# Quantising, a decay's scan, a weight load and gathers moved inside a joint pipeline of an eight-layer kernel

## The chip, the cores and the metric

The kernel runs on one core of a Trainium2 chip. The metric is device time in microseconds (us) for one execution; four runs of the kernel before gave 1078.79 to 1080.51 us, median 1079.82. The engines are TensorE (PE in the profile; PEld is its weight load), VectorE (DVE), ScalarE (ACT), GpSimd (POOL) and SyncE (SP, which issues most transfers). GpSimd issues the transfers of its own queue, among them the gathers by index.

## The reference, cut to what matters

The input `x` is 16 x 128 x 256: 16 sequences ("batches" b here) of 128 tokens with 256 features; `ctx` has the same shape. Four layers follow one another, each a cross-attention-like block and a feed-forward block, all with residuals and tanh gates. The change lies in the stretch from layer 1's attention to layer 2's first block, and in the load of the weights of layer 2's experts:

```python
def _L1_ffn_ref(x, w1, w2, w3):
    def act_quant(x):
        scale = 127.0 / jnp.clip(jnp.max(jnp.abs(x), axis=-1, keepdims=True), EPS)
        return jnp.clip(jnp.round(x * scale), -128.0, 127.0) / scale
    def weight_quant(w):
        scale = 1.0 / jnp.clip(jnp.mean(jnp.abs(w)), EPS)
        return jnp.clip(jnp.round(w * scale), -1.0, 1.0) / scale
    def bitlinear(x, w):
        return jnp.einsum('bsd,hd->bsh', act_quant(x), weight_quant(w))
    h = jax.nn.silu(bitlinear(x, w1)) * bitlinear(x, w3)
    return bitlinear(h, w2)

def _L2_xattn_ref(q, k, v, decay):          # k = v = ctx, q = layernorm(x)
    kv = kh * vh
    def step(r, inc):
        r = d * r + inc
        return (r, r)
    _, rs = jax.lax.scan(step, r0, kv_t)    # along the 128 tokens
    out = qh * jnp.moveaxis(rs, 0, 1)

x = x + jnp.tanh(g_ffn[0])   * _L0_ffn_ref(_layernorm(x), ...)      # 8 experts, top 2
x = x + jnp.tanh(g_xattn[1]) * _L1_xattn_ref(_layernorm(x), ctx, ctx, mask, Wq, Wk, Wv, Wo)
x = x + jnp.tanh(g_ffn[1])   * _L1_ffn_ref(_layernorm(x), w1, w2, w3)
x = x + jnp.tanh(g_xattn[2]) * _L2_xattn_ref(_layernorm(x), ctx, ctx, decay)
x = x + jnp.tanh(g_ffn[2])   * _L2_ffn_ref(_layernorm(x), ...)      # 8 experts, top 2
```

The weights w1 and w3 are 256 x 704, w2 is 704 x 256. Each is scaled by the mean of its absolute values, rounded and clipped to -1, 0 or 1. Since layer 2's keys and values are both `ctx`, its recurrence runs over the squares of `ctx`, with one decay per head of 16 channels.

## The kernel before, in words

Channels or tokens of one batch lie on 128 partitions. `xg` holds the running x, `ctxT` holds `ctx` with channels on partitions, as two halves c of 128 channels, each with 16 x 128 columns (batch after batch). The stages run in order: layer 0's block, its experts (`stage_moe0`), then a joint pipeline (`stage_l1x` with `following`), then layer 2's experts (`stage_moe2`) and layer 3.

**The joint pipeline** is the loop over n from -4 to 22 in `stage_l1x`. In step n it gathers the expert outputs of batch n+4 and takes its statistics (`stats`, which calls `collect`), normalises it, and runs the attention of batch n: queries (`tq`, L1041), scores (`s`, L1083), exponentials (`pt`, L1086), the mix with values (`av`, L1092; `avs`, L1094), and one step later `normalise` (transposes `ta`, L1100; the rows L1102 to L1105, which end with the tile `o`), `turn_o` (`to`, L1111; `oT`, L1113) and `output` (`y`, L1120; L1122). Two steps later the batch is done, and pairs q of two batches enter the following stages. The function `then(m, place)` is called at four places (0 to 3) of each step; the table `order` says which function of pair q runs at which place. A key (d, place) means step m = 3 + d + 2q. So pair q has statistics in step 3+2q at place 3 (L1294 to L1297, the power on GpSimd), scaling and the largest value in step 4+2q at place 0 (L1303 to L1315), rounding on ScalarE (`rounded`, L1320) at place 1, transposes (`fx`, L1328, L1329) at place 3, the two products with w1 and w3 in step 5+2q (`fu`, L1339; silu, L1346; L1347; L1356 to L1363), rounding and transposing of the hidden values in step 6+2q (L1367; `fh`, L1374; L1375), w2 in step 7+2q at place 2 (`fy`, L1381; L1386), and layer 2's block, `retain`, in step 8+2q (`fr`, L1401, transposes of ctxT; L1404, L1405).

**Preparation.** `follow` begins with the loads of w1, w3 and w2 as float32 into one tile `raws` (the slot of layer 0's expert weights), in whose rest GpSimd writes `dk[0]`, 2048 columns of ones with a zero at the start of each batch. `begun(n)` is called once in each step n >= 0, at its end but before place 3, and hands out the rest: step 0 lays out small buffers; steps 1 to 3 sum the absolute values of one weight each (`total`, L1236); steps 1 and 2 also square one half of ctxT on ScalarE (L1257); step 3 computes the scales (`size`: the matmul `ts`, L1240, over partitions and L1241 to L1243); step 4 quantises w1 and w3 and step 5 w2, with three VectorE operations for each (`integers`, L1251 to L1253); step 6 and step 7 each multiply `dk[0]` by the decay of one half (L1260) and scan that half in one operation over all 2048 columns (L1263), the zeros restarting it at each batch; step 8 issues the six loads of layer 2's expert weights (`moe2_weights`, L134 and L140) into the slot that `raws` gives up.

**Order.** TensorE, VectorE and ScalarE execute in the order in which the code is written (`manual_schedule`); GpSimd and SyncE get an order from the scheduler. Every engine takes its own instructions one after another. `fetcher` keeps three buffers `yc`; `collect(b)` asks for batch b and b+1, each by two indirect gathers on GpSimd's queue (L707), and adds them with L726.

Of the kernel before, what the change touches and what calls it, by code (L numbers as in the profile page):

```python
# [10 lines left out]
F32 = mybir.dt.float32  # L11
BF16 = mybir.dt.bfloat16
F32R = mybir.dt.float32r
AF = mybir.ActivationFunctionType
ALU = mybir.AluOpType
# [3 lines left out]
P = 128  # L19
B = 16  # L20
D = 256
# [34 lines left out]
def passage(ctx: ExitStack, tc: tile.TileContext, a: dict, out: bass.AP, inv, flag):  # L56
# [69 lines left out]

    def moe2_weights():

        t = mow.tile([P, (E + 1) * WE], F32R, name="L2we", tag="mw")
        v = t.rearrange("p (e w) -> p e w", e=E + 1)  # L130
        for n, s in ((0, "w1"), (1, "w3")):
            for c in range(2):
                at = (2 * c + n) * I
                nc.gpsimd.dma_start(  # L134
                    v[:, :, at : at + I], a[f"L2_{s}"][c * P : (c + 1) * P].rearrange("p (e i) -> p e i", e=E + 1)
                )
        w2 = a["L2_w2"]
        for n in range(2):
            at = 4 * I + n * D
            nc.gpsimd.dma_start(  # L140
                v[0:HI, :, at : at + D],
                bass.AP(tensor=w2.tensor, offset=w2.offset + n * HI * D, ap=[[D, HI], [I * D, E + 1], [1, D]]),
            )
        return t


    def layernorm(pool, g, extra=None, tag="xn"):
# [569 lines left out]
    def collector(pool, ys, pos, wgt):  # L717

        fetch = fetcher(pool, ys, pos, 3)

        def collect(b):
            y = fetch(b)
            fetch(b + 1)
            xv = xg[b // GB][:, b % GB, :]
            for i in range(2):
                nc.vector.scalar_tensor_tensor(xv, y[:, i, :], wgt[:, i, b : b + 1], xv, ALU.mult, ALU.add)  # L726

        return collect
# [440 lines left out]
    def following(sh, dcol):  # L1169
# [5 lines left out]

        def follow(pss, pst):


            raws = mow.tile([P, (E + 1) * WE], F32, name="raws", tag="mw")
            cut = [6 * D * i for i in range(4)]  # L1180
            flat = [raws[:, cut[i] : cut[i] + n * width] for i, (_, n, width) in enumerate(sizes)]
            for (name, n, width), raw in zip(sizes, flat):
                nc.sync.dma_start(
                    raw.rearrange("p (n w) -> p n w", n=n), a[f"L1_ffn_{name}"].rearrange("(n p) w -> p n w", p=P)
                )
            dk = [raws[:, cut[3] + i * B * P : cut[3] + (i + 1) * B * P] for i in range(2)]
            nc.gpsimd.memset(dk[0], 1.0)
            nc.gpsimd.memset(dk[0].rearrange("p (b s) -> p b s", b=B)[:, :, 0:1], 0.0)
            v = {}
            wq = []  # L1190

            def layout():

                t = sh.tile([P, 2 * B * P], F32, name="follow", tag="xT", bufs=1)
                at = [0]

                def take(name, n, *shape):
                    u = t[:, at[0] : at[0] + n]
                    at[0] += n
                    if shape:  # L1200
                        names = "abc"[: len(shape)]
                        u = u.rearrange(
                            f"p ({' '.join(names)}) -> p {' '.join(names)}", **{k: d for k, d in zip(names, shape)}
                        )
                    v[name] = u

                take("xn", 2 * D, 2, D)
                for i in range(2):
                    take(f"sil{i}", HID // 2)
                    take(f"hid{i}", 6 * P)  # L1210
                    nc.gpsimd.memset(v[f"hid{i}"][:, HID:], MAGIC)
                at0 = at[0]
                take("xT", 2 * P)
                v["xT"] = v["xT"].bitcast(BF16).rearrange("p (c s) -> p c s", c=2)
                for i in range(2):
                    take(f"hT{i}", 3 * P)
                    v[f"hT{i}"] = v[f"hT{i}"].bitcast(BF16).rearrange("p (n s) -> p n s", n=6)
                take("sum", 6, 3, 2)
                take("step", 3)
                take("s2t", 1)  # L1220
                take("magic", 2)
                for i, x in enumerate((MAGIC, -MAGIC)):
                    nc.gpsimd.memset(v["magic"][:, i : i + 1], x)
                for r in range(2):
                    for f in "fr":
                        take(f"st{f}{r}", 12, 2, 6)
                        take(f"mv{f}{r}", 4, 2, 2)
                        take(f"ve{f}{r}", 2)
                        take(f"rs{f}{r}", 2)
                    take(f"am{r}", 2)  # L1230
                    take(f"iv{r}", 2)
                    take(f"a13{r}", 4, 2, 2)
                    take(f"hm{r}", 6, 3, 2)
# [4 lines left out]
            def size():  # L1238
# [3 lines left out]
                nc.vector.reciprocal(v["sum"][:, :, 1], v["step"])  # L1242
                nc.vector.tensor_scalar(v["s2t"], v["step"][:, 2:3], tg[:, 5:6], 1.0 / 127.0, ALU.mult, ALU.mult)  # L1243

            def integers(i):
                name, n, width = sizes[i]
                if i == 2:
                    w = kv1.tile([P, n, width], BF16, name="w2q", tag="k3")
                else:
                    w = sh.tile([P, n, width], BF16, name=f"{name}q", tag="sil")  # L1250
                nc.vector.tensor_scalar(flat[i], flat[i], v["sum"][:, i, 1:2], MAGIC, ALU.mult, ALU.add)  # L1251
                nc.vector.tensor_scalar(flat[i], flat[i], MAGIC, 1.0, ALU.subtract, ALU.min)
                nc.vector.tensor_scalar(w.rearrange("p n w -> p (n w)"), flat[i], -1.0, None, ALU.max)  # L1253
                wq.append(w)

            def squared(c):
                nc.scalar.activation(ctxT[:, c, :], ctxT[:, c, :], AF.Square)  # L1257

            def decayed(c):
                nc.vector.tensor_scalar(dk[1], dk[0], dcol[:, c : c + 1], None, ALU.mult)  # L1260

            def scanned(c):
                nc.vector.tensor_tensor_scan(ctxT[:, c, :], dk[1], ctxT[:, c, :], 0.0, ALU.mult, ALU.add)  # L1263

            def begun(n):
                if n == 0:
                    assert not work
                    layout()
                elif n < 4:
                    total(n - 1)  # L1270
                    if n < 3:
                        squared(n - 1)
                    else:
                        size()
                elif n == 4:
                    integers(0)
                    integers(1)
                elif n == 5:
                    integers(2)
                elif n < 8:  # L1280
                    decayed(n - 6)
                    scanned(n - 6)
                elif n == 8:
                    l2we.append(moe2_weights())

            def x_of(q):
                b = 2 * q
# [108 lines left out]
            def retain(q):  # L1396
# [19 lines left out]
                (3, 1): [lambda q: turn_hidden(q, 0)],  # L1416
                (3, 2): [lambda q: turn_hidden(q, 1)],
                (4, 2): [down],
                (5, 0): [lambda q: stats(q, "r")],
                (5, 1): [retain_normal],  # L1420
                (5, 3): [retain],
# [511 lines left out]
    with tc.tile_pool(name="kv1", bufs=1) as kv1:  # L1933
        vbuf = kv1.tile([P, B, 4, 32], F32, name="v", tag="k0")
        ka = kv1.tile([P, B, P], F32, name="ka", tag="k1")
        anyk = kv1.tile([P, B], F32, name="anyk")
        stage_l0x(ka, vbuf, anyk)
        l0s = moe0_shared()
        l0g = col_chunks("l0g", a["L0_gw"], E)
        cn = sorter(kv1)  # L1940
        kept = pos, wgt, cn, xs, ys
        l1k = col_chunks("l1k", a["L1_wk"], P)
        l1v = col_chunks("l1v", a["L1_xattn_Wv"], 64)
        l1q = col_chunks("l1q", a["L1_wq"], 512)
        l1o = col_chunks("l1o", a["L1_xattn_Wo"], D)
        dcol = load("dcol", [P, 2], a["dcol"])
        l2g = col_chunks("l2g", a["L2_gw"], E)
        l2b = load("l2b", [P, E], a["L2_ffn_gate_b"].partition_broadcast(P))
        l3w = l3_weights()
        l3r = col_chunks("l3r", a["L3_wr"], E)  # L1950
        l3br = load("l3br", [P, E], a["L3_ffn_br"].partition_broadcast(P))
        with tc.tile_pool(name="mow", bufs=1) as mow:
            l0w = moe0_weights()

            l2we = []
            work = [
                lambda _, ps, p=p: keys_values(p, ps, ka, vbuf, anyk, l1k, l1v) for p in range(B // 2)
            ]
            with tc.tile_pool(name="sh", bufs=2) as sh:
                stage_moe0(l0w, *l0s, l0g, 4, sh, *kept, work)  # L1960
                with tc.tile_pool(name="yc", bufs=3) as yc:
                    stage_l1x(l1q, l1o, ka, vbuf, collector(yc, ys, pos, wgt), work, following(sh, dcol))
            stage_moe2(kv1, l2we[0], l2g, l2b, 6, *kept)
    with tc.tile_pool(name="l3fw", bufs=1) as fw:
        l3a = col_chunks("l3a", a["L3_A"], 512, fw)
        l3B = col_chunks("l3B", a["L3_B"], D, fw)
# [92 lines left out]
```

## Time and profile before

The times of one profiled execution and of the runs shown:

| what | us |
|---|---|
| median of four runs (1078.79 to 1080.51) | 1079.82 |
| the profiled execution | 1075.64 |
| its span, first to last instruction | 1073.9 |
| TensorE / VectorE / ScalarE / GpSimd busy in the span | 900.2 / 612.4 / 450.8 / 341.0 |
| row L1105 of the first step that writes it (n = 1) | starts 363.56 |
| the same row in step 4, 8, 12, 16 | 393.04, 456.41, 504.65, 547.01 |
| first row of layer 2's experts on VectorE (L750) | starts 582.06 |

In the page's second part the span is cut in 40 slices of 26.8 us; a digit is the busy share of an engine in tenths, and PEclk is the granted clock of TensorE in tenths of full speed. The joint pipeline lies in slices 13 to 21:

```profile
PE   3899978899999978788964858998169999998797
...
DVE  5988867322225568876778586444445555534442
ACT  1211024223322546467662242455257777882111
POOL 5766322643124322421011046550533332201000
PEclk9999989999999988899997557899579999997999
```

A row of the timeline gives its start and duration, engine, line and operation, then the tile written, the tiles read and the shape; in brackets stands how long the engine was idle before it and what ended the wait. A row of a group ends with busy time and the mean in ns of one instruction. "follow" is the tile of small buffers of `following`.

GpSimd's own rows, where the loads of layer 2's weights stand among small operations and gathers:

```profile
443.83 1.13 POOL L134 DMA_DIRECT2D L2we<-in_L_w_dram  x1 [8.60 <-DVE ctxT L1263]
445.01 0.73 POOL L1297 TENSOR_TENSOR follow<-follow,neghalf 128x2 f32<-128x2 f32 x1
445.71 1.05 POOL L134 DMA_DIRECT2D L2we<-in_L_w_dram  x1
...
453.87 2.11 POOL L140 DMA_DIRECT2D L2we<-in_L_w_dram  x2 [0.85 <-issue]
456.28 1.08 POOL L707 DMA_INDIRECT yc<-ys,pos  x1 [0.30 <-issue]
```

### The profile page before, as it was taken

Reading aid. Unit: us, or ns where it says so; the run is one execution under the profiler, and the core shown is the slowest. Engines: PE = TensorE matmul, PEld = TensorE weight load, DVE = VectorE, ACT = ScalarE, POOL = GpSimd, SP = SyncE. Lnnn points to the kernel's source line nnn. Section 1 sums busy time; section 2 is a strip of 40 time slices with the busy share of each in tenths; the row PEclk is TensorE's granted clock in tenths of the full one; section 3 lists DMA queues with packets and bytes.
Section 4 is the critical chain, followed back from the end, with each engine's and each line's share of the span. In section 5 each row is a group of like instructions: output and inputs, shape, how many; then the busy total and the mean of one; then the engine's idle time right before and its main releaser. Section 6 shows DMA issues by size and latency. Waiting matters only on the chain. (4 is left out here: it accounts for less than half of the span.)

```text
span 1073.9 us, 14873 instructions
## 1 busy us (share of the span) xinstructions
PE 900.2 (84%) x5212; PEld 600.1 (56%) x5212; DVE 612.4 (57%) x1528; ACT 450.8 (42%) x690; POOL 341.0 (32%) x387
## 2 busy tenths in 40 slices
PE   3899978899999978788964858998169999998797
PEld 1444456677778434454543757887145555555564
DVE  5988867322225568876778586444445555534442
ACT  1211024223322546467662242455257777882111
POOL 5766322643124322421011046550533332201000
PEclk9999989999999988899997557899579999997999
DMA  9100070233341100870000102352588787520000
GB/s 305 41 1 1 0 221 20 65 107 104 78 137 47 40 20 20 136 66 1 1 1 15 64 1 89 118 141 79 151 238 237 220 221 194 166 76 1 20 31 32
DMA packets 71401, 94.12 MB, mean 88 GB/s; under 512 B 9271, under 2 KB 63127, under 8 KB 69015
## 3 DMA queue, kind: packets, MB, share of 16 engines
q1 hardware_dynamic: 56952, 67.21, 21.0%
q0 software_dynamic: 14080, 23.78, 10.9%
q10 hardware_dynamic: 288, 2.10, 0.5%
q8 instruction: 45, 0.74, 0.3%
q14 instruction: 36, 0.29, 0.1%
HBM read 57.06 MB, written 33.55 MB: 84 GB/s over the span
## 5 line engine op out<-in xcount | busy, mean ns | idle before, releaser
L1661 ACT ACTIVATE pt<-s 128x1024 f32<-128x1024 f32 x128 | 126.4, 1023 | 33.0 <-PE s L1654 30.3
L707 POOL DMA_INDIRECT yc<-ys,pos x64 | 62.1, 970 | 94.5 <-DVE x L726 54.6
L295 PE MATMUL y<-kv,toep 128*128 128x512 f32 x192 | 85.7, 598 | 0.7 <-DVE toep L235 0.7
L1654 PE MATMUL s<-qa,ka 64*128 64x256 f32 x512 | 64.8, 334 | 7.5 <-ACT pt L1661 6.8
L1670 PE MATMUL av<-pt,v 128*32 128x256 f32 x1024 | 69.4, 389 | 0.1
L287 POOL TENSOR_TENSOR kv<-ctxT 128x1024 f32<-128x1024 f32 x32 | 60.1, 1899 | 27.5 <-PE y L295 27.5
L1654 PEld LDWEIGHTS s<-qa,ka 64*128 64x128 f32 x512 | 39.0, 190 | 46.2 <-issue 23.4
L1681 DVE COPY avs<-av 128x256 f32<-128x256 f32 x64 | 27.1, 423 | 64.6 <-PE av L1670 49.7
L295 PEld LDWEIGHTS y<-kv,toep 128*128 128x128 f32 x192 | 35.5, 190 | 42.8 <-issue 39.4
L614 PE MATMUL ub<-L0we,xbT 128*128 x160 | 50.7, 460 | 2.6 <-ACT xbT L605 2.6
L591 POOL DMA_INDIRECT xb<-xs,who x40 | 38.1, 952 | 43.4 <-PE tb L603 33.3
L910 PE MATMUL yb<-L2we,hT 88*128 (+1 forms) x224 | 42.0, 317 | 9.8 <-DVE hT L734 4.0
L845 POOL DMA_INDIRECT xb<-xs,who x40 | 38.0, 950 | 31.9 <-PE tb L857 20.9
L1561 POOL TENSOR_TENSOR hl<-f,hl 128x512 fp32r<-128x512 f32 x16 | 20.5, 1279 | 78.9 <-ACT hl L1560 78.9
L300 DVE TENSOR_TENSOR pr<-y,qT 128x1024 f32<-128x1024 f32 x32 | 39.0, 1222 | 11.2 <-PE y L295 9.4
L1083 PE MATMUL s<-qa,ka 18*128 18x512 f32 x128 | 37.4, 661 | 9.1 <-ACT follow L1375 9.1
L910 PEld LDWEIGHTS yb<-L2we,hT 88*128 88x128 f32 x224 | 34.1, 208 | 16.7 <-DVE hT L734 8.7
L475 PE MATMUL up<-L0s,xT 128*128 128x352 f32 x128 | 42.4, 476 | 0.0
L303 DVE TENSOR_REDUCE oT<-pr 128x128 f32<-128x1024 f32 x32 | 38.9, 1219 | 1.0
L1670 PEld LDWEIGHTS av<-pt,v 128*32 128x32 f32 x1024 | 26.9, 110 | 20.4 <-issue 0.8
L640 PE MATMUL yb<-L0we,hTb 88*128 x160 | 37.9, 379 | 0.0
L614 PEld LDWEIGHTS ub<-L0we,xbT 128*128 128x128 f32 x160 | 28.8, 190 | 15.5 <-ACT xbT L605 2.8
(384 smaller groups left out, 2032.5 us busy)
## 6 DMA issues: line engine op xcount, KB each, us to landing
scr<-hl SPq DMA_DIRECT2D x64, 256.0 KB
ys<-ysb SPq DMA_DIRECT2D x40, 256.0 KB
qa<-scr SPq DMA_DIRECT2D x32, 256.0 KB
ka<-scr SPq DMA_DIRECT2D x32, 256.0 KB
L2we<-in_L_w_dram POOLq DMA_DIRECT2D x6, 792.0 KB
L0we<-in_L_w_dram SPq DMA_DIRECT2D x6, 704.0 KB
xs<-xn SPq DMA_DIRECT2D x8, 512.0 KB
ctxT<-in_ctxT_dram ACTq DMA_DIRECT2D x2, 1024.0 KB
```

The source lines that it names most:

```text
L287: nc.gpsimd.tensor_tensor(t, bc(ch, 3, 8), bc(ch, 2, 8), ALU.mult)
L295: nc.tensor.matmul(y[:, ns], lhsT=T[:, h, d : d + P], rhs=kv[mc][:, ns], start=(mc == 0), stop=(mc == lc))
L300: nc.vector.tensor_tensor(pr, y.rearrange("p (b j i) -> p b j i", b=B, j=8), bc(qT[:, lc, :, hs], 2, 8), ALU.mult)
L303: nc.vector.tensor_reduce(oT[:, lc, :, hs], pr, AX.X, ALU.add)
L475: nc.tensor.matmul(t[:, n, 0 : 2 * I], lhsT=xT[:, c, b * P : (b + 1) * P], rhs=s13[:, c, n, :], start=(c == 0), stop=(c == 1),)
L591: nc.gpsimd.indirect_dma_start(out=xbs[s][:, i, :], out_offset=None, in_=xs, in_offset=bass.IndirectOffsetOnAxis(ap=who[:, 2 * s + i : 2 * ...
L614: nc.tensor.matmul(t[:, i, 0 : 2 * I], lhsT=xbT[:, i, c, :], rhs=we[:, bass.ds(regs[s][i] + c * 2 * I, 2 * I)], start=(c == 0), stop=(c == 1),
L707: nc.gpsimd.indirect_dma_start(out=got[b][:, i, :], out_offset=None, in_=ys, in_offset=bass.IndirectOffsetOnAxis(ap=pos[:, i, b : b + 1], ...
L910: nc.tensor.matmul(y[:, i, :], lhsT=hT[:, x, k, i, :], rhs=we[0:HI, bass.ds(at[i] + 4 * I + k * D, D)], start=(n == 0), stop=(n == 3),)
L1654: nc.tensor.matmul(s[:, h, jj, :], lhsT=ka[r, 2 * i + jj, sc * P : (sc + 1) * P], rhs=qa[r, 2 * i + jj, :], start=True, stop=True,)
L1661: nc.scalar.activation(pts[b, i][:, sc], s, AF.Exp)
L1670: nc.tensor.matmul(av[c : c + 32, :], lhsT=va[:, sc, 8 * h + 2 * i + jj, :], rhs=pt[:, sc, h, jj, :], start=(sc == 0), stop=(sc == 1),)
```

## The change

Four edits, all in the joint pipeline:

- *Quantising.* Steps 1 and 2 sum all three weights (two in step 1), and step 2 also computes the scales. The first of the three quantising operations (multiply by the scale, add MAGIC) moves from VectorE to ScalarE as `rounded_weight`, in steps 2, 3 and 4; the two that stay on VectorE run in steps 3, 4 and 5, one weight each.
- *The scan.* The decay pattern is a tile of its own, for two batches and both halves (512 columns), filled and multiplied by the decay on GpSimd in step 0. Squaring and scanning go by pairs of batches: `scanned(q)` squares and scans 256 columns of each half, in step 7+2q at place 3 (the new entry (4, 3) of `order`).
- *The load.* `moe2_weights` returns its six loads as functions; `begun` makes the tile in step 6 and calls one load in each of the steps 6 to 11.
- *Gathers.* `collect(b)` also asks for batch b+2.

```diff
     def moe2_weights():
...
+        loads = []
         for n, s in ((0, "w1"), (1, "w3")):
             for c in range(2):
                 at = (2 * c + n) * I
-                nc.gpsimd.dma_start(
-                    v[:, :, at : at + I], a[f"L2_{s}"][c * P : (c + 1) * P].rearrange("p (e i) -> p e i", e=E + 1)
+                loads.append(
+                    lambda to=v[:, :, at : at + I], src=a[f"L2_{s}"][c * P : (c + 1) * P]: nc.gpsimd.dma_start(
+                        to, src.rearrange("p (e i) -> p e i", e=E + 1)
+                    )
                 )
...
-        return t
+            loads.append(lambda to=v[0:HI, :, at : at + D], src=src: nc.gpsimd.dma_start(to, src))
+        return t, loads
...
             y = fetch(b)
             fetch(b + 1)
+            fetch(b + 2)
...
-            raws = mow.tile([P, (E + 1) * WE], F32, name="raws", tag="mw")
+            raws = mow.tile([P, 18 * D], F32, name="raws", tag="mw")
...
-            dk = [raws[:, cut[3] + i * B * P : cut[3] + (i + 1) * B * P] for i in range(2)]
-            nc.gpsimd.memset(dk[0], 1.0)
-            nc.gpsimd.memset(dk[0].rearrange("p (b s) -> p b s", b=B)[:, :, 0:1], 0.0)
...
+                dk = kv1.tile([P, 2, 2, P], F32, name="decay", tag="k2")
+                nc.gpsimd.memset(dk, 1.0)
+                nc.gpsimd.memset(dk[:, :, :, 0:1], 0.0)
+                for c in range(2):
+                    nc.gpsimd.tensor_scalar(dk[:, c], dk[:, c], dcol[:, c : c + 1], None, ALU.mult)
+                v["decay"] = dk
...
+            def rounded_weight(i):
+                nc.scalar.activation(
+                    flat[i], flat[i], AF.Identity, bias=v["magic"][:, 0:1], scale=v["sum"][:, i, 1:2]
+                )
+
             def integers(i):
...
-                nc.vector.tensor_scalar(flat[i], flat[i], v["sum"][:, i, 1:2], MAGIC, ALU.mult, ALU.add)
                 nc.vector.tensor_scalar(flat[i], flat[i], MAGIC, 1.0, ALU.subtract, ALU.min)
                 nc.vector.tensor_scalar(w.rearrange("p n w -> p (n w)"), flat[i], -1.0, None, ALU.max)
...
-            def squared(c):
-                nc.scalar.activation(ctxT[:, c, :], ctxT[:, c, :], AF.Square)
-
-            def decayed(c):
-                nc.vector.tensor_scalar(dk[1], dk[0], dcol[:, c : c + 1], None, ALU.mult)
-
-            def scanned(c):
-                nc.vector.tensor_tensor_scan(ctxT[:, c, :], dk[1], ctxT[:, c, :], 0.0, ALU.mult, ALU.add)
+            early = {
+                0: [layout],
+                1: [lambda: total(0), lambda: total(1)],
+                2: [lambda: total(2), size, lambda: rounded_weight(0)],
+                3: [lambda: integers(0), lambda: rounded_weight(1)],
+                4: [lambda: integers(1), lambda: rounded_weight(2)],
+                5: [lambda: integers(2)],
+            }
...
+                for f in early.get(n, ()):
+                    f()
+                if n == 6:
                     l2we.append(moe2_weights())
+                if n >= 6 and l2we[0][1]:
+                    l2we[0][1].pop(0)()
+
+            def scanned(q):
+                for c in range(2):
+                    u = ctxT[:, c, 2 * q * P : (2 * q + 2) * P]
+                    nc.scalar.activation(u, u, AF.Square)
+                    nc.vector.tensor_tensor_scan(
+                        u, v["decay"][:, c].rearrange("p b s -> p (b s)"), u, 0.0, ALU.mult, ALU.add
+                    )
...
                 (4, 2): [down],
+                (4, 3): [scanned],
                 (5, 0): [lambda q: stats(q, "r")],
...
-            stage_moe2(kv1, l2we[0], l2g, l2b, 6, *kept)
+            stage_moe2(kv1, l2we[0][0], l2g, l2b, 6, *kept)
```

## The prediction

> **What bounds the kernel now.** I first cut the span at the normalisation row of each joint step (L1105 on VectorE, written once in steps 1 to 16) and asked for engine busy time between the cuts. In the columns PE, PEld, DVE, ACT and POOL busy, granted clock, DMA, the lines below are steps 5 to 8 and then 10 and 11 (a line runs from the row of step n-1 to that of step n).
>
> ```profile
> 393.04:409.44 16.40, 11.40 (x51) 5.47 (x50) 13.16 (x29) 6.90 (x12) 2.83 (x4) 0.79 0.06 16
> 409.44:422.93 13.49, 11.91 (x52) 7.06 (x50) 9.68 (x28) 9.74 (x14) 4.41 (x7) 0.75 0.07 21
> 422.93:437.45 14.52, 11.64 (x70) 6.63 (x66) 14.14 (x26) 7.61 (x13) 2.81 (x4) 1.00 0.07 19
> 437.45:456.41 18.96, 12.36 (x52) 6.73 (x50) 14.77 (x34) 9.05 (x13) 9.82 (x13) 0.73 1.22 178
> ...
> 469.95:480.53 10.58, 9.25 (x52) 5.41 (x50) 8.65 (x32) 8.87 (x13) 3.02 (x6) 1.00 0.01 2
> 480.53:494.08 13.55, 12.06 (x74) 7.06 (x70) 10.34 (x28) 7.62 (x13) 0.84 (x2) 1.00 0.00 1
> ```
>
> Undisturbed, an even step takes 10.58 us and an odd one 13.55, nearly all TensorE at full clock. Steps 5 to 8 take 2.9, 2.9, 1.0 and 8.4 us more, and these hold the work that the change touches. Next, the timeline of VectorE and TensorE there, to see who waits:
>
> ```profile
> 382.24 0.35 PE L1240 MATMUL ts<-follow,ones 128*128 128x3 f32 x2 [1.67 <-DVE follow L1236]
> ...
> 396.32 0.46 PE L1339 MATMUL fu<-w1q,follow 128*128 128x352 bf16 x2 [2.37 <-DVE w1q L1253]
> ...
> 450.14 2.08 PE L1083 MATMUL s<-qa,ka 18*128 18x512 f32 x4 [6.07 <-ACT follow L1375]
> ```
>
> ```profile
> 437.79 1.28 DVE L1260 TENSOR_SCALAR raws<-raws,dcol 128x2048 f32<-128x2048 f32 x1
> 439.10 4.42 DVE L1263 TENSOR_TENSOR_SCAN ctxT<-raws,ctxT 128x2048 f32<-128x2048 f32 x1
> ```
>
> TensorE waits for the sums (382), for w1's integers (396; the next row, w3's, waits 2.17 more at 398.94), and 6.07 us while VectorE scans. Each is a serial piece put at the end of a step. Third, an even step with nothing extra, to see what a later VectorE costs there:
>
> ```profile
> 472.50 0.73 DVE L1303 TENSOR_SCALAR follow<-x,follow 128x256 f32<-128x256 f32 x2 [0.85 <-POOL follow L1297]
> ...
> 474.60 1.09 ACT L1320 ACTIVATE follow<-follow 128x256 f32<-128x256 f32 x2 [0.30 <-DVE follow L1312]
> ...
> 476.53 1.13 PE L1083 MATMUL s<-qa,ka 18*128 18x512 f32 x4 [0.68 <-ACT follow L1375]
> ```
>
> After an odd step's L1105 comes a chain with no slack: statistics, GpSimd's power (a gap of 0.85 us on VectorE), scaling, the largest value (L1312), rounding on ScalarE (it waits 0.30), L1375, TensorE's s (it waits 0.68). Whatever VectorE gets more there, beyond that gap, lengthens the step. Step 6 confirms it: the three operations of w2 (1.01 + 0.96 + 0.96 = 2.93 us) stand there and the step is 2.91 longer.
>
> **The change, part by part** (minus is time saved).
>
> Scans, removed. Step 7 loses L1260 and L1263 of channel half 0 (5.70 us, mostly in slack): its excess over step 9's 13.54, -1.0. Step 8 loses the other 5.70. There L1312 ends 10.73 us after L1105 against 4.62 in step 10 (6.1 us: the 5.70 and rows slowed beside GpSimd's issues), and from L1312 to the next L1105 it takes 8.23 against 5.96 (2.27 us at a clock of 0.50): -8.4. The two 128x2048 squares (1.90 us each) leave ScalarE in steps 1 and 2; only TensorE's 0.42 us wait for oT in step 2 goes with them: -0.4.
>
> Scans, added: 16 of 128x256 and 16 squares, two of each behind the statistics of every odd step from 7 to 21. No scan of this size is in the trace; two sizes that are (groups by line; the second number behind the bar is the mean in ns):
>
> ```profile
> L1263 DVE TENSOR_TENSOR_SCAN ctxT<-raws,ctxT 128x2048 f32<-128x2048 f32 x2 | 8.8, 4424 | 0.1
> ...
> L377 DVE TENSOR_TENSOR_SCAN cum<-ce,eq 128x128 f32<-128x128 f32 x4 | 1.7, 425 | 0.1
> ```
>
> Between 128 and 2048 a column costs (4.424 - 0.425)/1920 = 2.08 ns, so 256 cost 0.69 us; ends 0.43 (the 128 row) and 0.85 (two of those). Two, overlapped by 0.1 as neighbours on VectorE are, take 1.28. A square: the copy of 256 columns takes 0.38 and lets the next start after 0.25, L1320's 256 take 0.55; I take 0.37, ends 0.25 and 0.55. In steps 7, 9 and 11 the squares stand behind two exponentials, so the first starts where oT's copy did (471.72 in step 9) and ends at 471.72 + 0.37 = 472.09, the scans run to 473.35, and L1303 starts 0.85 later than its 472.50. Behind it are L1309 to L1312, for which ScalarE waits: +0.85 each in steps 8, 10 and 12. Steps 13 and 15 load no table between and have the exponentials sooner: by the same sum on 517.70 and 538.81, +0.63 each. In 17 the squares are early, 1.28 less the gap of 0.83: +0.45. In 19 and 21 the scans stand ahead of the statistics, in VectorE's unbroken last stretch: +2.5. Together 3 x 0.85 + 2 x 0.63 + 0.45 + 2.5 = +6.8; with the ends of scan and square 3 to 10. No table is loaded for a square (none was before L1257).
>
> Quantising. The sums (L1236, 1.61, 1.61, 1.74 us) now stand in steps 1, 1 and 2, the matmul ts in step 2. TensorE still waits for it, and behind it stand to, av and tq of step 3, which has no gap (7.66 of 7.67 us busy). VectorE is 0.35 late from the doubled sum, so ts issues near 374.95 where "to" began at 372.91: +2.3, ends 0 (if slack appears) and 4 (with a slow spell as at 382). Behind the first rounding on ScalarE (it waits for ts) stand oT, avs and xT, oT some 1.5 us late; y wants it only after av and tq (3.8 us), so nothing. Step 4 loses the sum, ts and the small rows behind (2.63 us to L1312 over step 10) and gets two w1 operations (2 x 0.89): -0.8. Rounding moves to ScalarE: by L1367 (704 columns 0.93) and L1320 (256: 0.55) a column costs 0.86 ns, so 1408 take 1.54 and 1536 take 1.65; ends 1.2 (at the square's 1.90 for 2048) and 1.7. In step 5 VectorE does two operations of w3 (1.79) instead of six (5.5), but w2's rounding delays L1329 from 393.97 to 395.55; TensorE's first fu pair then ends near 397.1, and the table load behind it starts at 397.2 instead of 399.77: -2.5. Step 6 has two operations for three: -1.0.
>
> Loads. raws no longer holds the decay, so its last reader is w2's quantiser in step 5. In the changed program GpSimd issues the parts (1.06 us each) between its small rows from step 6 on: three, then the step's power, one gather, three more, the next gather. The first part can start only when VectorE begins the statistics (1.4 us), so the power behind it is not late; cover gone, it would be 1.06 us in step 6. The parts need TensorE's L2we only at 612. Gathers: the third fetch gains almost nothing, since GpSimd already issued each gather when its buffer came free (row L707 waits for L726, 46.2 us in all), still the rule with three buffers. A gather now lies behind three parts in the queue: six took some 24 us (444 to 468), so about 12, and it is wanted over two steps (24 us) later: 0. The decay's memset and two multiplies on GpSimd lie near 339, where it waits for VectorE: 0, or about 1 us if not.
>
> Sum: -1.0 - 8.4 - 0.4 + 6.8 + 2.3 - 0.8 - 2.5 - 1.0 = -5.0.
>
> The clock. It drops after some gaps (TensorE's busy time and, third number from the end, its clock, by stretches of 2 us):
>
> ```profile
> 524.00:526.00 2.00, 1.73 (x10) 1.00 0.04 8
> 526.00:528.00 2.00, 2.00 (x7) 0.63 0.00 0
> ```
>
> That spell follows a wait of 1.15 us before s at 524.27 and stretches five groups of matmuls by 1.75 us; step 8's cost 2.27; gaps of 1.03 at 485 and 509 brought none. The change makes the gap before s in steps 8 to 12 longer (0.68 + 0.85, part of it moved ahead of fh) and moves ts's gap into a TensorE-bound step. I count one spell more that matters, 2.0 us (ends 0 and 5 spells): -3.0.
>
> The Trainium skill, "TensorE: Matmul & The Clock Gate", section "Why this matters for your kernels", asks only that idle gaps stay under about 3 us. By it no spell would come and the sum would stay -5.0; the spell after 1.15 us above speaks against it, so the row decides.
>
> The profiled execution took 1075.64 us around a span of 1073.9; the median of the four runs is 1079.82, 4.2 above. I take the same offset after: 1079.82 - 3.0 = 1076.8.
>
> **Rivals.**
> *Slow clock in every even step (slower).* The longer waits before s in steps 8, 10, 12 and 14, and ts in step 3, each bring a spell of about 2.0 us: -5.0 + 5 x 2.0 = +5.0, 1084.8. It decides from the third spell on (2.5 x 2.0 = 5.0). For it: 526. Against it: steps 9 to 13 show 1.00 throughout.
> *Step 3 takes the wait, no spell comes.* VectorE's chain hides ts as it did in step 4: -5.0 - 2.3 = -7.3, 1072.5. Against it: step 3 has no gap on TensorE.
> *The scans give the gain back.* Scan and square at their upper ends (+10 for +6.8) and one spell: +0.2, 1080. For it: no slack in the chain.
> *Gathers late behind the weights.* If a gather waited out all six parts (24 us), VectorE would stand at L726 for a few us: 1080 or more. The distance of two steps speaks against it.
>
> **How the numbers follow.** Forecast 0.34, no stall in step 3 0.20, gain given back 0.24, slow clock 0.19, gathers 0.03. What this kernel's measurement can tell from no change is 0.2%, 2.2 us. Faster: the first two, 0.53 with a little of the forecast's edge taken off; same 0.25, slower 0.22. The forecast's own range is 1074.5 to 1078.5; with the others until two in ten are out, 1071 to 1083.
>
> **What would show it.** Step 8 near 11.4 us without a 6 us wait; step 5 near 13.9; L1303 of even steps 0.85 late; ts waiting in step 2 and step 3 near 10. I am wrong if the granted clock is below 1.00 in two or more of steps 9 to 13, if L726 waits for a gather, or if the scans take much over 0.7 us.

## The result and the profile after

The changed kernel took 1077.5 us (median of 52 runs, 1073.26 to 1082.34) where the kernel before took 1078.86 on the same chip (78 runs, 1074.71 to 1083.47). The ratio is 0.9986 with a 95% interval of 0.9979 to 0.9993: 1.4 us faster, at most 2.3. The profiled execution took 1078.72 us around a span of 1076.9, which is 3.0 us longer than the span of before. The stretch that the change touches, from row L1108 of step 1 (L1105 before) to the first VectorE row of layer 2's experts, is nevertheless shorter: 217.56 us against 218.50. The other 3.9 us lie outside the change, 1.0 ahead of that stretch and most of the rest behind 650 us, and single executions of one kernel differ by as much in the runs above. So the account below is made over the joint pipeline, step by step, with the same cuts as before.

The slices of the page first, VectorE's busy tenths and the granted clock:

```profile
DVE  5988866322225556787788585444445555535342
...
PEclk9999989999999979999986567999579999998899
```

In slices 15 to 17 (digits 6, 8, 8 before) VectorE is now at 5, 6, 7: the long scans and three of the quantising operations have left it. The clock falls in slice 15 (8 before, 7 now) and is back at 9 in 16 and 17 (8 before): the slow spell of step 8 is gone, and step 3, which had none, has one.

The busy time by step, cut at L1108; columns as before. The lines are steps 3 to 6, then 8, 9 and 10:

```profile
373.69:384.13 10.44, 8.21 (x36) 4.78 (x36) 5.89 (x19) 4.82 (x7) 2.53 (x3) 0.84 0.09 27
384.13:397.23 13.10, 10.63 (x40) 5.80 (x38) 8.57 (x26) 6.22 (x10) 4.39 (x7) 0.75 0.07 20
397.23:412.61 15.38, 12.20 (x58) 5.92 (x54) 9.56 (x25) 8.43 (x12) 2.83 (x4) 0.88 0.06 18
412.61:425.51 12.90, 10.42 (x50) 5.87 (x50) 9.17 (x26) 9.75 (x14) 8.28 (x11) 0.87 1.41 205
...
439.07:451.56 12.49, 10.33 (x57) 6.00 (x56) 9.68 (x33) 9.43 (x15) 5.02 (x8) 1.00 0.19 37
451.56:464.55 12.99, 11.18 (x67) 6.44 (x65) 10.35 (x29) 7.57 (x13) 0.85 (x2) 1.00 0.00 0
464.55:475.96 11.41, 10.49 (x52) 5.89 (x50) 9.81 (x33) 9.48 (x15) 3.03 (x6) 0.85 0.01 1
```

Step 8 went from 18.96 to 12.49 us and its clock from 0.73 to 1.00: by far the largest gain. Step 10, at 11.41 against 10.58, pays for two scans. Steps 3 to 6 run at clocks of 0.75 to 0.88. Steps 4 to 6 had slow spells before, too (clocks of 0.87, 0.79 and 0.75); step 3 is the one that had none. These are its line and that of step 4 of before:

```profile
372.35:380.02 7.67, 7.66 (x38) 3.71 (x34) 5.31 (x15) 5.12 (x7) 2.53 (x3) 1.00 0.12 36
380.02:393.04 13.02, 10.38 (x48) 5.46 (x44) 8.79 (x29) 4.84 (x9) 4.37 (x7) 0.87 0.07 20
```

Step 3 took 7.67 us and takes 10.44. TensorE's rows at the waits of the prediction:

```profile
375.92 0.35 PE L1244 MATMUL ts<-follow,ones 128*128 128x3 f32 x2 [2.70 <-DVE follow L1240]
...
377.76 3.36 PE L1044 MATMUL tq<-xT,l1q 128*128 128x256 f32 x8
...
392.09 3.78 PE L1044 MATMUL tq<-xT,l1q 128*128 128x256 f32 x8 [2.39 <-ACT xT L1035]
```

The matmul ts waits 2.70 us for the sums, and behind it the eight matmuls tq of step 3 take 3.36 us; those of step 4 take 3.78 behind a wait of 2.39. The same eight take 1.99 at full clock. In step 8 the wait of 6.07 us before s is down to 0.91, and the two scans stand ahead of L1308 as forecast:

```profile
446.49 1.13 PE L1086 MATMUL s<-qa,ka 18*128 18x512 f32 x4 [0.91 <-ACT follow L1380]
```

```profile
441.29 1.28 DVE L1287 TENSOR_TENSOR_SCAN ctxT<-decay,ctxT 128x256 f32<-128x256 f32 x2 [0.52 <-ACT ctxT L1286]
442.48 0.71 DVE L1308 TENSOR_SCALAR follow<-x,follow 128x256 f32<-128x256 f32 x2
```

### The profile page after: what moved, and what is told of

The parts are those of the page before. It is cut to its first block, busy times and chain, and to the rows that moved or that the text cites. A ratio compares the mean times of both kernels' runs of the same rounds, so it can differ in the third digit from the quotient of the medians.

```text
span 1076.9 us, 14892 instructions
## 1 busy us (share of the span) xinstructions
PE 900.2 (84%) x5212; PEld 600.4 (56%) x5212; DVE 608.3 (56%) x1537; ACT 456.6 (42%) x707; POOL 342.1 (32%) x389
## 5 line engine op out<-in xcount | busy, mean ns | idle before, releaser
L913 PE MATMUL yb<-L2we,hT 88*128 (+1 forms) x224 | 42.2, 316 | 10.4 <-issue 4.1
```

What stands on the lines that cost most here:

```text
L913: nc.tensor.matmul(y[:, i, :], lhsT=hT[:, x, k, i, :], rhs=we[0:HI, bass.ds(at[i] + 4 * I + k * D, D)], start=(n == 0), stop=(n == 3),)
```

## The experiments

All ratios are to the kernel before on the same chip, with 95% intervals. Four chips were used, e1 to e4 on one, e5 to e8, e9 to e11 and e12 on others; on these the kernel before takes 1067 to 1069 us. The rows before and after are those of the comparison above. The sums of step lengths are of each run's own profile, in us.

| kernel | ratio | steps 2-6 | steps 7-16 | tail behind 16 |
|---|---|---|---|---|
| before | 1 | 59.37 | 124.08 | 35.05 |
| after | 0.9986 [0.9979, 0.9993] | 60.95 | 118.99 | 37.62 |
| e5 after again | 0.9969 [0.9948, 0.9989] | 62.79 | 118.95 | 37.59 |
| e1 quantising alone | 1.0009 [0.9991, 1.0027] | 59.10 | 124.63 | 38.19 |
| e2 scan alone | 0.9961 [0.9945, 0.9977] | 60.85 | 118.99 | 37.62 |
| e3 load and gathers undone | 0.9962 [0.9945, 0.9980] | 60.00 | 118.78 | 37.61 |
| e4 scan moved | 0.9945 [0.9926, 0.9964] | 60.03 | 115.25 | 36.77 |
| e6 ts filled | 0.9945 [0.9924, 0.9966] | 58.23 | 119.48 | 38.18 |
| e7 quantising in the gaps | 0.9877 [0.9858, 0.9896] | 51.96 | 117.93 | 38.25 |
| e8 e4 and e7 | 0.9847 [0.9827, 0.9866] | 50.97 | 115.76 | 38.54 |
| e9 rounding of w2 sooner | 0.9968 [0.9950, 0.9987] | 61.69 | 119.52 | 38.21 |
| e10 sums sooner | 0.9920 [0.9895, 0.9945] | 54.75 | 120.20 | 40.03 |
| e11 four gather buffers | 0.9942 [0.9925, 0.9958] | 63.02 | 117.48 | 38.77 |
| e12 e8 and e11 | 0.9851 [0.9834, 0.9869] | 50.79 | 114.75 | 39.06 |

The tail scatters: in e1, whose tail has the same work as before, it is 38.19 us at clocks down to 0.54, against 35.05. Readings below rest on the steps.

**e1: quantising alone.** The kernel before, with `rounded_weight`, `integers` and the `early` table of after for them; squares and scans of whole halves stay in steps 1, 2, 6 and 7, the six loads in step 8.

```diff
...
+                    1: [lambda: total(0), lambda: total(1), lambda: squared(0)],
+                    2: [lambda: total(2), size, lambda: rounded_weight(0), lambda: squared(1)],
+                    3: [lambda: integers(0), lambda: rounded_weight(1)],
+                    4: [lambda: integers(1), lambda: rounded_weight(2)],
+                    5: [lambda: integers(2)],
...
```

> Before, with the quantising of after and nothing else of the change (squares, decays, scans, load and gathers as before). Theory (quantising is a net loss): in the trace of after steps 2 to 6 took 0.34 + 2.77 + 0.08 - 1.02 - 0.59 = +1.6 us against before, so this kernel is 1.5 to 2 us slower than before, ratio 1.0015, with TensorE waiting 2.7 us for ts at the end of step 2. Rival (the working of the prediction, +2.3 - 0.8 - 2.5 - 1.0 = -2.0 us): ratio 0.998.

The time can't tell it from no change. By the steps: 2 +0.34, 3 +2.35, 4 -0.43, 5 -1.49, 6 -1.04, together -0.27 us. What steps 4 to 6 save, steps 2 and 3 spend. The prediction's price of -2.0 us (0.998) lies outside the interval. Step 3 is longer here without a slow spell, at a clock of 1.00: TensorE waits 2.01 us for the sums, and y waits 0.97 more for oT, which stands on ScalarE behind the rounding and a square of 1.89 us that the kernel after doesn't have there. So e1 prices quantising together with that square; e3 against e2, below, prices it without.

**e2: the scan alone.** After, with quantising, loads in code and gathers as before.

```diff
...
+                1: [lambda: total(0)],
+                2: [lambda: total(1)],
+                3: [lambda: total(2), size],
+                4: [lambda: integers(0), lambda: integers(1)],
                 5: [lambda: integers(2)],
...
```

> Before, with the scan by pairs of after and nothing else (three operations a weight, one sum a step, six loads in step 8, gathers of two batches). Theory (the scan is where the whole gain is): steps 7 and 8 lose about 1.0 and 6.5 us, steps 10, 12, 14 and 16 gain 0.84, 0.84, 0.6 and 0.6, the stretch behind step 16 gains 2.6, oT's wait in step 2 (0.4) goes: about -2.5 to -3.5 us, ratio 0.997. Rival (the load's earlier start is what frees step 8): step 8 stays above 16 us and the ratio is 1.000 or more.

Every step from 7 to 16 is within 0.01 us of after's. The measured gain of the whole change is all here: 0.9961 alone, 0.9969 for everything (e5), and the intervals overlap. Step 2 is 0.68 shorter than before without the squares (0.4 forecast). One step is longer than before, step 6 by 2.14 us. The three operations of w2 stood there before as well; new are the loads, beside which two rows of VectorE take 0.46 us more, and a slow spell right behind s, which waits 2.51 us: tq takes 3.31 instead of 1.99. For the loads run in step 6 here, too, although their calls stand in step 8 (e3 says why). So the rival, that their leaving step 8 is what freed it, isn't tested by this run. The rows of before speak against it: L1312 ended 6.1 us later in step 8 than in step 10, and 5.70 of these were L1260 and L1263.

**e3: loads and gathers as before.**

```diff
-            fetch(b + 2)
...
-                if n == 6:
-                    l2we.append(moe2_weights())
-                if n >= 6 and l2we[0][1]:
-                    l2we[0][1].pop(0)()
+                if n == 8:
+                    l2we.append(moe2_weights())
+                    for f in l2we[0][1]:
+                        f()
```

> After, with all six loads issued in step 8 and gathers of two batches, as before. Theory (these two edits are worth nothing): within 0.7 us of after, ratio to before 0.9986 again; no L729 waits for a gather in either. Rival (the spread load or the sooner gathers carry the gain): about 1.4 us slower than after, ratio 1.000.

No gain of after is lost: 0.9962. It can't be told from the 0.9961 of the scan alone on the same chip, so the new quantising, by which the two differ, is worth nothing measurable either. GpSimd's rows say why; first those of e3, then those of after:

```profile
416.45 1.13 POOL L137 DMA_DIRECT2D L2we<-in_L_w_dram  x1 [4.02 <-DVE w2q L1260]
...
425.80 1.05 POOL L137 DMA_DIRECT2D L2we<-in_L_w_dram  x1
426.83 2.17 POOL L145 DMA_DIRECT2D L2we<-in_L_w_dram  x2
```

```profile
415.19 1.13 POOL L137 DMA_DIRECT2D L2we<-in_L_w_dram  x1 [4.02 <-DVE w2q L1261]
...
424.56 1.05 POOL L137 DMA_DIRECT2D L2we<-in_L_w_dram  x1
425.59 2.18 POOL L145 DMA_DIRECT2D L2we<-in_L_w_dram  x2
```

The six loads begin in step 6 in both, behind the last reader of `raws` and in the same order. What freed them was the scan's edit, which took the decay pattern out of `raws`; in e1, where the scan still reads it, they stay in step 8. Six calls in six steps change nothing that the engine does: the edit "load" is a rewording. The same comparison settles the third fetch.

**e4: the scan moved.** After, with the squares behind `turn_hidden` at (3, 2) and the scans at (3, 3) behind `retain`, one step sooner.

```diff
...
-                (3, 2): [lambda q: turn_hidden(q, 1)],
+                (3, 2): [lambda q: turn_hidden(q, 1), squared],
                 (4, 2): [down],
-                (4, 3): [scanned],
...
                 (5, 3): [retain],
+                (3, 3): [scanned],
```

> After, with the squares of pair q behind the second hidden transpose of step 6+2q (place 2) and its scans behind retain at place 3 of that step, where VectorE waits 1.6 us for the silu of the next. Theory (after an odd step's L1108 VectorE has no slack, elsewhere it has): steps 8 to 16 even lose 0.84, 0.84, 0.84, 0.6, 0.6 us, the last stretch 1 to 1.5, together about -5 us against after, ratio to before 0.994. Rival (the 0.84 us go with the scan wherever it stands, or ScalarE's squares cost): within 1 us of after, 0.9986.

Steps 8, 10 and 12 are 0.83, 0.84 and 0.85 us shorter than e3's, 14 and 16 0.60 and 0.59; the odd steps keep their length (step 15 within 0.2). So the scans cost what they stand in front of: in an even step's chain 0.84, in an odd step, where TensorE sets the length, nothing. The time doesn't show it yet: 0.9945 and the 0.9962 of e3 have overlapping intervals, and of the 5 us expected the steps give 3.5 and the tail 0.8.

**e5: after again**, unchanged, beside e6 to e8 on their chip.

> After itself, beside the three below on one chip. Every theory: ratio to before 0.9986, within 0.998 to 0.9995. If it comes out near 0.996, the first comparison undersold the change and the two undone edits of e3 are worth nothing.

The ratio is 0.9969 where the first comparison gave 0.9986. That is below the range expected and nearer to 0.996; the intervals overlap, so it isn't shown that the first comparison undersold the change. Steps 7 to 16 repeat within 0.01 us; steps 3 and 5 don't (11.80 and 15.86 us against 10.44 and 15.38): the slow spells there vary from execution to execution.

**e6: TensorE kept busy before ts.** Nine matmuls of constants into the tile `ts`, ahead of the two that fill it.

```diff
-                t = pst.tile([P, 3], F32, name="ts", tag="a")
+                t = pst.tile([P, P], F32, name="ts", tag="a")
+                for _ in range(9):
+                    nc.tensor.matmul(t, lhsT=ones, rhs=ident, start=True, stop=True)
+                t = t[:, 0:3]
```

> After, with nine matmuls of constants (ones by ident, 128x128) into ts's tile ahead of ts, which fill the 2.7 us that TensorE waits for the last sum; nothing else waits on them. Theory (the wait brings the slow clock behind it): the spell at 376 to 382 is gone, tq of step 3 takes 1.99 instead of 3.36 us, step 3 is 1.4 us shorter. Rival (the spell comes from the phase of the clock's window or from something else): step 3 stays at 10.4 us.

Step 3 of e6 by windows, and TensorE's rows in it:

```profile
372.18:380.90 8.72, 8.33 (x52) 5.33 (x50) 5.88 (x17) 4.81 (x7) 2.52 (x3) 1.00 0.10 30
```

```profile
374.31 0.38 PE L1247 MATMUL ts<-follow,ones 128*128 128x3 f32 x2 [0.39 <-DVE follow L1240]
...
375.89 1.99 PE L1044 MATMUL tq<-xT,l1q 128*128 128x256 f32 x8
```

The matmul ts issues 2.13 us after the cut, against 2.23 in after: it waits for the sums as long as before. Yet the clock stays at 1.00, tq takes 1.99, and the step is 8.72 us instead of 10.44 (11.80 in e5). Of the 2.77 us by which the change lengthened step 3, 1.7 are the clock and 1.05 the wait itself. The spell is not that of a single execution: in the profiles of after, e3, e4, e5, e9 and e11, whose work in step 3 is the same, that step has a clock of 0.71 to 0.84 each time. The rival, that step 3 stays at 10.4 us, is out. (In the time, 0.9945 and the 0.9969 of e5 have overlapping intervals.)

**e9: the rounding of w2 sooner.** After, with this one operation behind xT of step 4.

```diff
-                4: [lambda: integers(1), lambda: rounded_weight(2)],
+                4: [lambda: integers(1)],
...
+            between = {(4, 2): [lambda: rounded_weight(2)]}
...
```

> After, with the rounding of w2 on ScalarE placed behind xT of step 4 instead of at the end of that step. Theory (step 5 fell short of its price because ScalarE does this 1.66 us before L1334 and TensorE's first hidden product waits 2.45 us for it): in step 5 L1334 comes some 1.5 us sooner, the wait before fu falls to about 1, step 5 from 15.4-15.9 to about 13.7, the rest as after: 1.5 to 2 us in all, ratio to the kernel before 0.995. Rival (step 5 is long because of the slow clock of step 4's wait alone): step 5 stays above 15.

The first fu waits 0.41 us instead of 2.45, but step 5 only goes to 14.50: the slow spell of step 4 reaches into it. And the 0.9 gained there was lost again, with 0.7 more, one step later:

```profile
399.24 0.77 PE L1343 MATMUL fu<-w1q,follow 128*128 128x352 bf16 x2 [0.41 <-ACT follow L1333]
...
419.25 1.13 PE L1086 MATMUL s<-qa,ka 18*128 18x512 f32 x4 [2.22 <-ACT follow L1379]
420.31 3.63 PE L1044 MATMUL tq<-xT,l1q 128*128 128x256 f32 x8
```

In after the spell of step 6 begins earlier, at av, where VectorE's chain sets the pace; here it falls on tq, right behind the wait before s, and step 6 takes 14.53 us instead of 12.90. So step 5 ends between the theory's 13.7 and the rival's 15: the wait for w2's rounding costs 0.9, and the slow clock, the rival's cause, the larger part, as e10 shows next. The kernel is no faster than after (0.9968; e5 has 0.9969).

**e10: the sums sooner.** One sum in each of steps 0, 1 and 2; ts and the first rounding behind the mix of step 3.

```diff
-                0: [layout],
-                1: [lambda: total(0), lambda: total(1)],
-                2: [lambda: total(2), size, lambda: rounded_weight(0)],
+                0: [layout, lambda: total(0)],
+                1: [lambda: total(1)],
+                2: [lambda: total(2)],
...
+            between = {(3, 1): [size, lambda: rounded_weight(0)]}
...
```

> After, with the sums in steps 0, 1 and 2, and the scales' matmul and the first rounding behind the mix of step 3; all other quantising where it is in after. Theory (steps 2 and 3 pay for the wait of TensorE on the sums and for the clock behind it): step 2 8.1 and step 3 7.9 us, ts waits for nothing; step 4 keeps its wait of 2.4 us before tq and its clock, 12 to 13 us; step 5 as in after. 3.5 us less in all, ratio 0.9935. Rival (the wait moves on to the next piece of the preparation): step 4 grows by what steps 2 and 3 save.

Steps 2 to 5 of e10 by windows, and TensorE's rows:

```profile
364.98:373.09 8.11, 8.11 (x42) 4.09 (x38) 5.27 (x16) 3.88 (x6) 2.52 (x3) 1.00 0.11 33
373.09:380.98 7.89, 7.88 (x40) 3.93 (x36) 5.79 (x18) 4.87 (x7) 2.53 (x3) 1.00 0.12 35
380.98:393.07 12.09, 9.57 (x46) 4.54 (x42) 8.38 (x26) 6.08 (x10) 4.40 (x7) 1.00 0.07 22
393.07:406.83 13.76, 10.96 (x50) 5.25 (x50) 9.56 (x24) 8.46 (x13) 2.83 (x4) 0.88 0.07 20
```

```profile
375.74 0.38 PE L1244 MATMUL ts<-follow,ones 128*128 128x3 f32 x2
...
388.94 1.99 PE L1044 MATMUL tq<-xT,l1q 128*128 128x256 f32 x8 [2.40 <-ACT xT L1035]
```

Now ts waits for nothing, and steps 2 and 3 fall to 8.11 and 7.89 as expected. The wait before tq of step 4 is unchanged (2.40), but no spell comes with it, and steps 4 and 5 fall by 1.01 and 1.62 as well, with their work as in after: the first fu of step 5 still waits 2.32 us. That was not expected ("step 4 keeps its wait ... and its clock"). The rival, that the wait moves on, is out.

**e7: quantising in the gaps.** e10, with w1's two operations in step 4 behind the attention's statistics, w2's rounding behind xT of step 4, and both other weights' operations at the end of step 4.

```diff
...
+                3: [lambda: rounded_weight(1)],
+                4: [lambda: integers(1), lambda: integers(2)],
...
+                (3, 1): [size, lambda: rounded_weight(0)],
+                (4, 1): [lambda: integers(0)],
+                (4, 2): [lambda: rounded_weight(2)],
...
```

> After, with one sum each in steps 0, 1 and 2, ts and the first rounding in step 3 at place 1, w1's integers in step 4 at place 1 (VectorE waits 2.4 us there), w2's rounding in step 4 at place 2, and w3's and w2's integers at the end of step 4 (VectorE waits 5.4 us then). Theory (only work behind an odd step's L1108, and TensorE's wait for ts, lengthen steps): step 2 -0.3, step 3 -2.7, step 4 -2, step 5 -1.5 to -2, step 6 -2, about -8 us against after. Rival (the steps 2 to 6 are held by clock spells wherever the work stands): less than -4 us.

Steps 2 to 6: 8.11, 7.88, 11.12, 12.91, 11.94, together 9.0 us less than in after, where 8 were expected; the rival (less than 4) is out. The wait before tq of step 4 is 0.65 us, that before the first fu of step 5 is 0.77. Against e5 on the same chip this placement is worth 0.92%, some 9.8 us, with the same instructions.

**e8: e4 and e7 together.**

> The edits of e4 and e7 together. Theory: they touch different steps and add up, -5 and -8 us, about -13 us against after, ratio to before 0.986. Rival (they share a bound): no better than the better of the two.

1050.73 us against 1068.27 on this chip: the two gains add up as far as the intervals tell. Those of e8 and e7 overlap.

**e11: four buffers for the gathers.**

```diff
-        fetch = fetcher(pool, ys, pos, 3)
+        fetch = fetcher(pool, ys, pos, 4)
```

> After, with four buffers for the gathered rows instead of three, so that the gather of the last batch is issued in step 7 and no gather stands ahead of the power of step 8. Theory (step 8 is 1.08 us over step 10 because VectorE's L1026 waits 1.77 us for GpSimd's L1017 behind two gathers): L1026 waits at most 0.7, step 8 11.4, step 9 up to 13.5, so 0.5 us in all, ratio as after within its interval. Rival (step 8 is held by the two scans, not by the gather): step 8 stays at 12.5.

In after step 8 is 1.08 us longer than step 10 at a clock of 1.00. GpSimd's and VectorE's rows of after there:

```profile
446.99 1.08 POOL L709 DMA_INDIRECT yc<-ys,pos  x1 [0.23 <-DVE x L729]
448.37 0.96 POOL L709 DMA_INDIRECT yc<-ys,pos  x1 [0.30 <-issue]
449.35 0.60 POOL L1017 TENSOR_TENSOR rs<-ve,neghalf 128x1 f32<-128x1 f32 x1
```

```profile
449.99 0.41 DVE L1026 TENSOR_SCALAR xn<-x,mv,rs 128x256 f32<-128x256 f32 x1 [1.77 <-POOL rs L1017]
```

The last batch's two gathers stand ahead of the power, and VectorE waits 1.77 us for it. With a fourth buffer (e11's steps 8 and 9):

```profile
439.31:450.72 11.41, 9.25 (x52) 5.40 (x50) 9.81 (x34) 9.48 (x15) 3.03 (x6) 1.00 0.15 22
450.72:464.28 13.56, 12.07 (x74) 7.07 (x70) 10.34 (x29) 7.63 (x13) 0.85 (x2) 1.00 0.00 0
```

Step 8 is 11.41 and step 9 13.56, both as expected: the gathers cost 1.08 us and half of it came back in step 9, whose TensorE work had been started sooner. The ratio is below what these 0.5 us explain. Its interval overlaps those of e5 and of e9 (on the same chip), not that of the first comparison; the pipeline's own length shows no more, so the rest stays open.

**e12: all three.**

> e8_both_moved with four buffers for the gathered rows. Theory: the parts add up, since they lie in different steps: steps 2 to 7 as in e8, step 8 10.57 (e8 11.64), step 9 13.55 (12.98), so 0.5 us less than e8, ratio 0.984. Rival (the nearest thing takes the place of each wait): steps 2 to 16 no shorter than e8's 166.7.

Steps 8 and 9 came out at 10.58 and 13.56, and steps 2 to 16 at 165.54 us against e8's 166.73. In the time it can't be told from e8: 0.9851 and 0.9847. Either version takes 1.5% less than the kernel before, and they are the fastest here.

## Why the prediction was right or wrong

The forecast was 1076.8 us, 3.0 less than before; measured were 1077.5 and 1.4 less. The sign and most mechanisms held. That the time came out within 0.7 us is partly luck: the kernel before measured 0.96 us under the median that the forecast started from, which made up for more than half of the 1.6 us that the gain fell short. On another chip (e5) the same change gained 0.31%, 3.3 us. The pipeline of the profiled execution lost 0.94 us where the sum said 3.0. Here are the terms beside what the profile of after shows; where a slow spell lay in a step, the runs that had none there (e6 for step 3, e10 for steps 4 and 5) give its length at full clock, and the rest is put under the clock. Step 5 of e10 still has a spell, behind its first fu, so its figure is an upper bound. Before had slow spells of its own in steps 4 and 5, and no run shows these steps of before without them. So the rows of steps 4 and 5 set a step without a spell, or nearly so, against one with it, and only the sum of the rows of steps 3 to 5 and of the clock is a like comparison: +1.0 forecast, +1.83 measured.

| term | forecast | measured |
|---|---|---|
| step 2, squares gone, sums doubled | -0.4 | +0.34 |
| step 3, wait for ts | +2.3 | +1.05 (8.72 in e6, less 7.67) |
| step 4 | -0.8 | -0.93 (12.09 in e10, less 13.02) |
| step 5 | -2.5 | -2.64 (13.76 in e10, less 16.40) |
| step 6 | -1.0 | -0.59 |
| step 7 | -1.0 | -0.96 |
| step 8, scan out, two in | -7.55 | -6.47 |
| step 9 | 0 | -0.55 |
| steps 10, 12 | +0.85 each | +0.83, +0.84 |
| steps 14, 16 | +0.63 each | +0.59, +0.60 |
| tail | +2.95 | +2.57 |
| slow clock (forecast: one spell more; measured: steps 3 to 5 of after) | +2.0 | +4.35 (1.72 + 1.01 + 1.62) |
| sum | -3.0 | -0.94 (0.03 in steps 11, 13, 15) |

*The scan was right.* The interpolated 0.69 us for 256 columns, 1.28 for two, is the measured row (1.28; 0.676 alone), the square took 0.41 for 0.37, and the price of each even step is the forecast one within 0.04 us. e4 showed the reason that was given: the chain behind the statistics has no slack. The tail's term agrees too, but e1 shows a tail 3.1 us longer without any such work, so it isn't shown.

*The clock: the count held, the rest only in part.* "I count one spell more that matters, 2.0 us": after has slow spells in steps 3 to 6, before had them in 4 to 6. The new one, in step 3, is the one more, and without it (e6) the step is 1.72 us shorter. What the term didn't hold is the cost of the spells that remain, which now fall on tq of step 4 and run into step 5: in e10, without the one at tq, the same work takes 1.01 and 1.62 us less. What the spells of before cost in these steps is not known, so 4.35 us are what three spells of after cost, not what the change added. The forecast looked for new ones before s in steps 8 to 14; step 10 got one, and it cost nothing: 11.41 us at a clock of 0.85 in after and 11.41 at 1.00 in e3. The bounds given (0 to 5 spells) held the value.

*Step 3 was half right.* TensorE has to wait, as forecast, and the rival "step 3 takes the wait" is out. But "no gap (7.66 of 7.67 us busy)" was no proof of no slack: in the row of av, busy time contains the pipelined waiting for pt. In e6, where it begins late, av takes 1.06 us against 1.82 in step 3 of before, and the step grows by 1.05, not 2.3.

*Steps 2, 6 and 8 were mis-sized by side effects.* Of the 2.1 us by which the sum missed, step 8 holds 1.08, steps 3 to 5 with the clock 0.83, step 2 0.74 and step 6 0.41; step 9 and the tail gave back 0.55 and 0.38. In step 2 the doubled sum does lengthen the step: without it e2 has 8.11, with it after has 9.13, 1.02 more; the forecast had put its 0.35 us only into step 3. In step 6, L1308 takes 1.08 us beside a load's issue (two on 0.73 before) and L1301 0.28 for 0.17, together 0.46, which covers the missing 0.41; e1, whose loads stay in step 8, has these rows at 0.73 and 0.17 and a step shorter by 1.04, as forecast. The prediction had seen the same rows slowed in step 8 of before and gave them no price in step 6. "The first part can start only when VectorE begins the statistics (1.4 us), so the power behind it is not late" was true (the gap is 0.86) and overlooked the operations beside it. In step 8 "gathers ... 0" was wrong: once the loads were gone from step 8's queue, the last gathers came ahead of the power, and e11 gives the price, 1.08 in step 8 less 0.57 in step 9. With them out of the way step 8 takes 11.41 us, which is the forecast -7.55.

*What did nothing* was forecast as nothing: the third fetch and the loads in parts (e3). The prediction had named what lets the loads start, that `raws` no longer holds the decay; e3 shows that this alone decides, wherever the calls stand.

*The rivals.* "The scans give the gain back" (1080) and "slow clock in every even step" (1084.8) are out by the steps; no gather made L729 wait. Quantising, which the sum priced at -2.0 from step 3 to 6 without the clock, brought nothing that can be measured: e1 can't be told from before, nor e3 from e2, and e7 shows that the same instructions elsewhere are worth 9.8 us.

## What to carry to other kernels

Price a serial piece by the engine that stands still for it, and then by what that engine does next: the wait of 2.7 us for ts cost 1.05 us, the slow clock behind it 1.7. Spread work goes into the step where the waiting engine has something else to do, not simply to an earlier step; the same quantising instructions were worth nothing in one placement and 0.9% in another. Before a call is moved on a queue whose order the scheduler makes, look for the buffer that releases it, since here that alone decided when the loads ran, and their departure brought the gathers ahead of a small operation on the path.

## What the runs showed of the hardware

Whether a slow spell of the clock came did not follow from the length of a gap alone. Gaps of 2.70 (ts), 2.39 (tq of step 4) and 2.45 us (fu) each came with one in after, while the same gap before tq, 2.40 us, brought none in e10. In e9 two gaps of 0.85 and 0.83 us in step 6 brought none, where 1.07 and 0.83 at the same place brought one in after. The Trainium skill, "TensorE: Matmul & The Clock Gate", section "Why this matters for your kernels", asks only that idle gaps stay under about 3 us; no gap named here is as long, so that limit would not have warned of these. The same page's Part 1 says that the window in which activity is counted has some 3.4 us and runs freely, whatever the kernel does; that could let one gap bring a spell and an equal one none, as seen here, but no run here measured the window.

A spell cost time where TensorE set the length of the step, and nothing in step 10, where it didn't: that step took 11.41 us at a clock of 0.85 (after) and at 1.00 (e3), while tq of step 3, 1.99 us at full clock, took 3.36 and the step 1.7 more. Nine matmuls of constants during the wait kept the clock at 1.00 and saved 1.7 us of step 3 (e6), though the engine got no work done sooner.
